# Bias weights of the sampled position bias put on diagonals of TensorE's stationary matrices

## The chip, the cores and the metric

The kernel runs on one core of a Trainium2 chip. A core has a matrix engine (TensorE, PE in the profile; PEld are its weight loads), a vector engine (VectorE, DVE), an activation engine (ScalarE, ACT), a general engine (GpSimd, POOL) and a queue engine for transfers (SyncE, SP). Each engine works through its own list of instructions in order; semaphores order them against each other. The metric is the time of one execution on the device in microseconds, the median over runs; lower is better. One further execution was taken with the hardware profiler, and durations and waits come from that one.

## The reference, cut to what matters

The reference is two layers on a tensor of 4 x 32 x 32 x 384: a deformable attention, then a linear attention with a mixture of experts. Only the deformable attention's bias and softmax matter here. With 4 batches, 6 heads of 64 channels, and n = 1024 positions, each key position has an offset, and the bias is a bilinear sample of a learned table around it:

```python
attn = jnp.einsum('bmhc,bnhc->bhmn', qh, k) * scale
disp = (ref.reshape(1, n, 1, 2) - pos.reshape(Bq * G, 1, n, 2)) * 0.5
bias = _bilinear_sample(rpe_img, disp)          # four neighbours, four weights
attn = jax.nn.softmax(attn + bias, axis=-1)
out = jnp.einsum('bhmn,bnhc->bmhc', attn, v)
# in _bilinear_sample:
top = tl + ax * (tr - tl)
bot = bl + ax * (br - bl)
out = top + ay * (bot - top)
```

For one key position the fractional parts `ax` and `ay` are the same for all 1024 queries. So the whole bias row of a key is a window of 33 x 33 values of the upsampled table, with one weight for its upper rows, one for its lower rows, one for the left columns and one for the right columns:

bias[y, x] = wl * t[y, x] + wr * t[y, x + 1], with t[y, x] = wu * win[y, x] + wd * win[y + 1, x].

## The kernel before, in words

Keys lie on the 128 partitions, queries along the free dimension. A unit is one batch and head (24 in all); its 1024 keys are 8 blocks of 128, worked two at a time. A pair of blocks is called p (96 in all, 4 per unit, `KP = 4`), its place in the unit is `p % KP`, and the blocks in the pair are e = 0 and e = 1. The loop `for g in range(NP + 7)` runs a software pipeline over pairs, with kp = g % 4; in one turn it works on several pairs at once:

- `fetch_windows` (L1168): GpSimd gathers the 128 windows of a block with an indirect transfer, for pair g + 4.
- `upper` (L1184, ScalarE) and `lower` (L1194, VectorE) make t, 128 x (32 x 33), for pair g + 2. There are four buffers for t.
- `left` (L1202, ScalarE) writes o = wl * t[:, :, 0:32], a 128 x 1024 tile, for pair g + 2.
- `scores` (L1221 and L1226, TensorE) for pair g + 1, in two steps. A step covers one half of one block and of the other. Its matmuls work on 64 x 64 tiles of the array: two tiles off the diagonal hold keys and multiply queries, two on the diagonal hold an identity and add o to the same PSUM bank group. PSUM holds one such tile ps of 128 x 2 x 1024, so the next pair's scores wait until this one has been read. Between the steps stands a small ScalarE copy (`turn_over`, L1241), which orders the second quarters behind the first.
- `right` (L1252, VectorE) for pair g + 1: for each half e, S[:, e] = wr * t[:, :, 1:33] + ps[:, e], from PSUM to SBUF.
- `running` (L1270, VectorE) keeps the running maximum over the pairs of a unit; the last pair adds a maximum of the two halves (L1272). `highest` and `spread` (L1282, L1286, L1298, L1306) turn that maximum into a row: transposes on TensorE (pm), a reduction on VectorE (nm), transposes again (pb), a copy on ScalarE (pbs).
- `minus` (L1311, VectorE) and `weights_of` (L1315, ScalarE, the exponential) for pair g - 4; `values` (L1329 and L1338, TensorE) for pair g - 5.
- `out_of` (L1354, ScalarE, kp = 0) evacuates a unit's output; `to_queries` (L1372 to L1388) and `to_channels` (L1405, L1412, in units of odd head) turn and normalise it; `project` (L1429, L1438, L1441) multiplies by the output weights, in kp = 0 and kp = 2. In the first units `last_pieces` (L257 to L295) puts what is left of the keys and values of later batches in the same places.

The order of the instructions on TensorE, ScalarE, VectorE and GpSimd in this stage is the order in which these calls are written (`tc.manual_schedule`); waits are derived from the tiles that instructions read and write. In one turn VectorE runs: running maximum (or, for kp = 0, the two `lower`), minus, the two `lower`, the two `right`. ScalarE runs: two `upper`, the copy of `turn_over`, the exponential, then the two av copies in kp = 0, then the two `left`.

Stages ahead of this one (norm, convolution, offsets, sampling, keys and values, tables) are ordered by a planner; stages after it are the linear attention and the experts. The change is in this one alone.

Of the kernel before, what the change touches and what calls it, by code (L numbers as in the profile page):

```python
# [11 lines left out]
F32 = mybir.dt.float32  # L12
I32 = mybir.dt.int32
AF = mybir.ActivationFunctionType
# [5 lines left out]
P = 128  # L20
B, HI, WI, NC = 4, 32, 32, 384
# [3 lines left out]
G, GC = 6, 64  # L25
# [126 lines left out]
def bc(ap, axis, n):  # L152

    dims = [list(d) for d in ap.ap]
    dims.insert(axis, [0, n])
    return bass.AP(ap.tensor, ap.offset, dims)
# [3 lines left out]
def body(  # L160
# [8 lines left out]
    nc = tc.nc  # L169
# [11 lines left out]
    ident = const.tile([P, P], F32, tag="ident", name="ident")  # L181
# [60 lines left out]
    x0 = early.tile([P, NB, NC], F32, tag="x0", name="xr0")  # L242
# [58 lines left out]
    with tc.tile_pool(name="a_w", bufs=1) as aw, tc.tile_pool(name="a_1", bufs=1) as a1, tc.tile_pool(  # L301
        name="a_2", bufs=2
    ) as a2, tc.tile_pool(name="a_3", bufs=2) as a3, tc.tile_pool(name="a_s", bufs=2) as asm, tc.tile_pool(
        name="a_cv", bufs=1, space=PSUM
    ) as pcv, tc.tile_pool(name="a_mm", bufs=2, space=PSUM) as pmm, tc.tile_pool(
        name="a_tr", bufs=3, space=PSUM
# [13 lines left out]
        step = plan.step  # L320
# [379 lines left out]
        os_ = {}  # L700
# [222 lines left out]
        for b in range(B):  # L923
# [56 lines left out]
            for f in range(2):  # L980
# [22 lines left out]
                for i, n in enumerate(sizes):  # L1003
                    k0, r = K4 * f + i * n, n / K4
# [109 lines left out]

    with tc.tile_pool(name="b_w", bufs=1) as bwp, tc.tile_pool(name="b_qkv", bufs=2) as bq, tc.tile_pool(
        name="b_win", bufs=4
    ) as bwin, tc.tile_pool(name="b_t", bufs=4) as bt, tc.tile_pool(name="b_o", bufs=2) as bo_, tc.tile_pool(
        name="b_s", bufs=6
    ) as bS, tc.tile_pool(name="b_m", bufs=2) as bm, tc.tile_pool(name="b_ao", bufs=1) as bao, tc.tile_pool(
        name="b_y", bufs=3  # L1120
# [2 lines left out]
        nc.sync.dma_start(wo, w_out.rearrange("(a p) d -> p a d", p=P))  # L1123
        bo = bwp.tile([P, NC], F32, tag="bo", name="bo")
        nc.sync.dma_start(bo, bc(b_out, 0, P))
        units = [(b, h) for b in range(B) for h in range(G)]
        ao = {}
        heads = {}

        HALF = [slice(e * GC, (e + 1) * GC) for e in range(2)]  # L1130
        FULL = [slice(f * 512, (f + 1) * 512) for f in range(2)]
        SYNC = mybir.DependencyInfo(mybir.DependencyClass.Sync, mybir.DependencyReason.DATA)
        KP = NB // 2
        NP = KP * len(units)

        def load_qk(u):


            b, h = u
            c, r0 = h // 2, (h % 2) * GC  # L1140
            q = bq.tile([P, N], F32, tag="q", name=f"q{b}_{h}")
            k = bq.tile([P, NB, GC], F32, tag="k", name=f"k{b}_{h}")
            ks = k_d[b][c][r0 : r0 + GC, :].rearrange("p (a e j) -> p a e j", e=2, j=GC)
            for e in range(2):
                nc.sync.dma_start(q[HALF[e], :], q_d[b][c][r0 : r0 + GC, :])
                nc.sync.dma_start(k[HALF[e]], ks[:, :, 1 - e, :])
            return q, k
# [9 lines left out]


        wins, ts, os_, pss, Ss, turns = {}, {}, {}, {}, {}, {}
        qk, vs, ms, nms, pbss, pos, avs = {}, {}, {}, {}, {}, {}, {}  # L1160

        def fetch_windows(p):
# [13 lines left out]
        def weight(p, e, i):  # L1176
            b, h = units[p // KP]
            return bw[b][:, 2 * (p % KP) + e, h, i : i + 1]
# [19 lines left out]
        def left(p, e):  # L1198

            if p < NP:  # L1200
                o = bo_.tile([P, HI, WI], F32, tag="o", name=f"o{p}_{e}")
                nc.scalar.activation(o, ts[p, e][:, :, 0:WI], AF.Copy, scale=weight(p, e, 2))  # L1202
                os_[p, e] = o.rearrange("p y x -> p (y x)")

        def scores(p, step):


            if p >= NP:
                return
            i, kp = divmod(p, KP)  # L1210
            if step == 0:
                if kp == 0:
                    qk[i] = load_qk(units[i])
                pss[p] = bps.tile([P, 2, N], F32, tag="s", name=f"ps{p}")
            q, k = qk[i]
            ps = pss[p]
            e, d = 1 - step, step
            made = []
            for f in range(2):
                for r in range(2):  # L1220
                    made.append(nc.tensor.matmul(  # L1221
                        ps[HALF[1 - r], e, FULL[f]], k[HALF[r], 2 * kp + e, :], q[HALF[r], FULL[f]],
                        start=(step == 0), stop=(step == 1),
                    ))
                for r in range(2):
                    made.append(nc.tensor.matmul(  # L1226
                        ps[HALF[r], d, FULL[f]], ident[HALF[r], HALF[r]], os_[p, d][HALF[r], FULL[f]],
                        start=(step == 0), stop=(step == 1),
                    ))
            if step == 0:  # L1230
                turns[p] = made
            else:
                for i_ in made:
                    tc.add_manual_dep(i_.ins, turns[p].ins.name, SYNC, reason="second quarters")
                del turns[p]
# [10 lines left out]
        def right(p):  # L1246

            if p < NP:
                ps = pss.pop(p)
                st = bS.tile([P, 2, N], F32, tag="S", name=f"S{p}")  # L1250
                for e in range(2):
                    nc.vector.scalar_tensor_tensor(  # L1252
                        st[:, e, :].rearrange("p (y x) -> p y x", x=WI),
                        ts.pop((p, e))[:, :, 1:WIN],
                        weight(p, e, 3),
                        ps[:, e, :].rearrange("p (y x) -> p y x", x=WI),
                        ALU.mult,
                        ALU.add,
                    )
                    del os_[p, e]  # L1260
                Ss[p] = st
# [236 lines left out]
        with tc.manual_schedule(  # L1498
# [9 lines left out]
            for p in range(2):  # L1508
                for e in range(2):
                    upper(p, e)  # L1510
                    lower(p, e)
                    if p == 0:
                        left(p, e)
                fetch_windows(p + 2)
            scores(0, 0)
            turn_over(0)
            scores(0, 1)
            for e in range(2):
                left(1, e)
            right(0)  # L1520
            for g in range(NP + 7):


                i, kp = divmod(g, KP)
                values(g - 5, 0)
                scores(g + 1, 0)
                for e in range(2):
                    upper(g + 2, e)
# [30 lines left out]
                for e in range(2):  # L1559
                    if kp:  # L1560
                        lower(g + 2, e)
                    left(g + 2, e)
                fetch_windows(g + 4)
                if kp % 2 == 0:
                    project(1)
                right(g + 1)
                if g == 15 * KP:
                    load_early()
# [7 lines left out]
            while waiting:  # L1576
                tag, n = spots.pop(0)
# [152 lines left out]
    with tc.tile_pool(name="c_1", bufs=1) as c1, tc.tile_pool(name="c_2", bufs=2) as c2, tc.tile_pool(  # L1730
        name="c_s", bufs=2
# [320 lines left out]
    with tc.tile_pool(name="d_w1", bufs=1) as dw1, tc.tile_pool(name="d_s1", bufs=1) as ds1, tc.tile_pool(  # L2052
        name="d_w2", bufs=1
    ) as dw2, tc.tile_pool(name="d_s2", bufs=1) as ds2, tc.tile_pool(name="d_2", bufs=2) as d2p, tc.tile_pool(
        name="d_h", bufs=3
# [94 lines left out]
        for t in range(-2, len(units)):  # L2150
# [12 lines left out]
            d = ds[j]  # L2163
# [59 lines left out]
```

## Time and profile before

| quantity | value |
|---|---|
| median of 3 runs | 2853.29 us (2848.89 to 2854.21) |
| the profiled execution | 2848.2 us, span of its instructions 2846.1 us |
| TensorE busy | 2586.8 us, 91% |
| VectorE busy | 1579.4 us, 55% |
| ScalarE busy | 1157.8 us, 41% |
| GpSimd busy | 855.1 us, 30% |
| mean granted TensorE clock | 0.968 of full |
| attention stage, first scores to last `right` | about 388 to 1365 us |

The shares are averages over stages with different limits: in the stage of the experts, from about 1800 us to the end, TensorE is busy nearly all the time and VectorE little; in the attention stage VectorE is the busiest. So the page's totals don't say what a change to the attention is worth; the rows of that stretch do. In the lines that follow, "x8" after a group is the number of instructions, the two figures in front are start and duration in us (timelines) or total busy us and mean ns (groups), and a bracket at the end gives the idle time before and who ended it. A float32 matmul makes two records.

### The profile page before, as it was taken

To read this page: it belongs to the slowest core of one execution; us is meant where nothing else is said; L and a number is where in the kernel's file an instruction comes from. 1 tells how busy PE (TensorE), PEld (TensorE's weight loads), DVE (VectorE), ACT (ScalarE), POOL (GpSimd) and SP (SyncE) were. 2 spreads that over 40 slices of the span, in tenths; PEclk is the share of its full clock that TensorE was granted. 3 is DMA by queue.
4 is the path that set the end of the run, shared out by engine and by line. 5 is a ranking of instruction groups with operands and counts; after the bars stand their busy time and mean duration, and the time that the engine had idled before them with its cause. 6 is when DMAs were issued, how large, how long until landed. Compare 5 with 4: busy or idle time off the path is not lost. (4 is left out here: it accounts for less than half of the span.)

```text
span 2846.1 us, 33342 instructions
## 1 busy us (share of the span) xinstructions
PE 2586.8 (91%) x12731; PEld 1283.8 (45%) x12731; DVE 1579.4 (55%) x2349; ACT 1157.8 (41%) x1532; POOL 855.1 (30%) x776
## 2 busy tenths in 40 slices
PE   8899938898989988888799898999999999999999
PEld 5455512332333333233365554555555555555566
DVE  3888859999999999999656765000101011011011
ACT  5565536777667766676323322111111111111121
POOL 1668863232333333332112335211112111021121
PEclk9899969999999999999999999999999999999999
DMA  7934575454546555544121312622223433374371
GB/s 205 257 114 132 175 208 165 130 154 146 164 145 195 176 157 149 145 151 127 55 74 51 120 45 70 250 103 103 103 103 118 147 129 140 115 255 172 117 267 59
DMA packets 267899, 404.77 MB, mean 142 GB/s; under 512 B 134674, under 2 KB 207634, under 8 KB 267356
## 3 DMA queue, kind: packets, MB, share of 16 engines
q1 hardware_dynamic: 214912, 230.43, 25.6%
q0 software_dynamic: 52112, 172.15, 18.7%
q8 instruction: 100, 1.64, 0.2%
q14 instruction: 59, 0.48, 0.1%
q10 hardware_dynamic: 716, 0.07, 0.0%
HBM read 345.68 MB, written 70.06 MB: 146 GB/s over the span
## 5 line engine op out<-in xcount | busy, mean ns | idle before, releaser
L2070 PE MATMUL ph<-d_xT,w 128*128 128x512 f32 (+1 forms) x1152 | 484.1, 554 | 1.3 <-ACT h L2077 1.3
L2102 PE MATMUL acc<-w,h 128*128 128x384 f32 x1392 | 480.3, 486 | 0.0
L1168 POOL DMA_INDIRECT win<-table,widx x192 | 280.2, 1459 | 640.3 <-DVE t L1194 608.5
L1221 PE MATMUL ps<-q,k 64*64 64x512 f32 x1536 | 382.1, 611 | 90.7 <-DVE S L1252 43.6
L2077 ACT ACTIVATE h<-ph,b1c 128x512 f32<-128x512 f32 (+1 forms) x192 | 124.1, 647 | 776.3 <-PE ph L2070 761.7
L1226 PE MATMUL ps<-o,ident 64*64 64x512 f32 x1536 | 378.4, 612 | 9.5 <-ACT o L1202 9.5
L2102 PEld LDWEIGHTS acc<-w,h 128*128 128x128 f32 x1392 | 264.1, 190 | 208.5 <-issue 73.2
L2070 PEld LDWEIGHTS ph<-d_xT,w 128*128 128x128 f32 x1152 | 217.0, 191 | 196.3 <-issue 144.5
L2132 POOL DMA_INDIRECT out<-rows,ei x67 | 67.1, 1002 | 700.2 <-DVE rows L2129 691.4
L871 POOL DMA_INDIRECT ga<-img,pidx x192 | 233.5, 1216 | 145.7 <-DVE gd L600 62.5
L1315 ACT ACTIVATE S<-S 128x2048 f32<-128x2048 f32 x96 | 183.4, 1910 | 190.3 <-DVE S L1311 190.3
L1221 PEld LDWEIGHTS ps<-q,k 64*64 64x64 f32 x1536 | 99.2, 134 | 355.4 <-issue 211.5
L1722 DVE COPY d_xT<-e_tr 128x512 f32<-128x512 f32 (+2 forms) x75 | 36.6, 512 | 386.1 <-PE e_tr L1719 386.1
L1194 DVE SCALAR_TENSOR_TENSOR t<-win,bw,t 128x1056 f32<-128x1056 f32 x192 | 244.7, 1316 | 5.9 <-ACT t L1184 4.6
L1252 DVE SCALAR_TENSOR_TENSOR S<-t,bw,ps 128x1024 f32<-128x1024 f32 x192 | 237.1, 1277 | 18.9 <-PE ps L1226 16.0
L2121 DVE SCALAR_TENSOR_TENSOR rows<-b2r,en,rows 128x384 f32<-128x384 f32 x67 | 40.9, 618 | 359.9 <-DMA rows<-out,ei 321.1
L1184 ACT ACTIVATE t<-win,bw 128x1056 f32<-128x1056 f32 x192 | 218.1, 1168 | 39.2 <-DMA win<-table,widx 38.1
L1202 ACT ACTIVATE o<-t,bw 128x1024 f32<-128x1024 f32 x192 | 212.8, 1144 | 37.0 <-DVE t L1194 30.1
L1329 PE MATMUL po<-S,v 128*64 128x512 f32 x768 | 199.1, 642 | 24.4 <-ACT av L1354 13.9
L1311 DVE TENSOR_TENSOR S<-S,pbs 128x2048 f32<-128x2048 f32 x96 | 219.0, 2283 | 2.1 <-ACT pbs L1306 2.1
L2129 DVE SCALAR_TENSOR_TENSOR rows<-acc,en,rows 128x384 f32<-128x384 f32 x67 | 41.4, 618 | 218.2 <-PE acc L2102 216.3
L1270 DVE TENSOR_TENSOR m<-m,S 128x2048 f32<-128x2048 f32 x48 | 117.1, 2440 | 1.6
(350 smaller groups left out, 3442.0 us busy)
## 6 DMA issues: line engine op xcount, KB each, us to landing
w<-in_L_ffn_w SPq DMA_DIRECT2D x50, 2304.0 KB
img<-in_x SPq DMA_DIRECT2D x48, 256.0 KB
q<-q_d SPq DMA_DIRECT2D x48, 256.0 KB
x<-in_x SPq DMA_DIRECT2D x8, 768.0 KB
q_d<-qt SPq DMA_DIRECT2D x24, 256.0 KB
v_d<-qkvw SPq DMA_DIRECT2D x32, 192.0 KB
v<-v_d SPq DMA_DIRECT2D x24, 256.0 KB
k<-k_d SPq DMA_DIRECT2D x48, 128.0 KB
```

Source lines behind the costliest of these rows:

```text
L871: nc.gpsimd.indirect_dma_start(out=ga[:, g].rearrange("p s c -> p (s c)"), out_offset=None, in_=img[b][:, :], in_offset=bass.IndirectOffse ...
L1168: nc.gpsimd.indirect_dma_start(out=win, out_offset=None, in_=tables[h // 2][:, :], in_offset=bass.IndirectOffsetOnAxis(ap=widx[b][:, nb, h ...
L1184: nc.scalar.activation(t.rearrange("p y x -> p (y x)"), wins[p, e][:, : HI * WIN], AF.Copy, scale=weight(p, e, 0),)
L1194: nc.vector.scalar_tensor_tensor(tf, wins.pop((p, e))[:, WIN:], weight(p, e, 1), tf, ALU.mult, ALU.add)
L1202: nc.scalar.activation(o, ts[p, e][:, :, 0:WI], AF.Copy, scale=weight(p, e, 2))
L1221: made.append(nc.tensor.matmul(ps[HALF[1 - r], e, FULL[f]], k[HALF[r], 2 * kp + e, :], q[HALF[r], FULL[f]], start=(step == 0), stop=(step ...
L1226: made.append(nc.tensor.matmul(ps[HALF[r], d, FULL[f]], ident[HALF[r], HALF[r]], os_[p, d][HALF[r], FULL[f]], start=(step == 0), stop=(ste ...
L1252: nc.vector.scalar_tensor_tensor(st[:, e, :].rearrange("p (y x) -> p y x", x=WI), ts.pop((p, e))[:, :, 1:WIN], weight(p, e, 3), ps[:, e, : ...
L1311: nc.vector.tensor_tensor(Ss[p], Ss[p], bc(pbss[p // KP][:, :], 1, 2), ALU.add)
L1329: nc.tensor.matmul(pos[i][0][HALF[f], :], vs[i][:, 2 * kp + e, :], Ss[p][:, e, FULL[f]], start=(first and e == 0), stop=(last and e == 1),)
L2070: nc.tensor.matmul(ph if short(d) else ph[:, :n], a, m, start=(c == 0), stop=(c == CK - 1))
L2102: nc.tensor.matmul(d["acc"][0 if short(d) else s][:, :NC], h[:, s * P : (s + 1) * P], d["w2"][:, hc, :], start=(hc == 0), stop=(hc == HC - 1),
```

## The change

The weight wl is no longer multiplied into t by ScalarE. Instead ScalarE writes a 128 x 64 tile whose diagonals (one per half of the partitions) hold wl, from a folded identity `fold`; TensorE uses that tile as the stationary matrix in place of the identity, and t itself, read with 32 columns of each row of 33, as the moving one. In two blocks of the eight of a unit (`WHOLE`: block e = 1 of the pairs 1 and 3) the right columns go the same way, with a second diagonal tile of wr and two more matmuls per half; there `right` is a plain ScalarE copy from PSUM to S instead of the VectorE instruction. The pool of the o tiles has six buffers instead of two. `fold` is made by two GpSimd copies ahead of the stage.

```diff
-        name="b_win", bufs=4 ... tc.tile_pool(name="b_o", bufs=2) as bo_
+        name="b_win", bufs=4 ... tc.tile_pool(name="b_o", bufs=6) as bo_
+        fold = bwp.tile([P, GC], F32, tag="fold", name="fold")
+        for e in range(2):
+            nc.gpsimd.tensor_copy(
+                fold[e * GC : (e + 1) * GC, :], ident[e * GC : (e + 1) * GC, e * GC : (e + 1) * GC]
+            )
+        WHOLE, rights = ((1, 1), (3, 1)), {}
         def left(p, e):
             if p < NP:
-                o = bo_.tile([P, HI, WI], F32, tag="o", name=f"o{p}_{e}")
-                nc.scalar.activation(o, ts[p, e][:, :, 0:WI], AF.Copy, scale=weight(p, e, 2))
-                os_[p, e] = o.rearrange("p y x -> p (y x)")
+                os_[p, e] = diagonal(p, e, 2)
+                if (p % KP, e) in WHOLE:
+                    rights[p, e] = diagonal(p, e, 3)
+        def diagonal(p, e, i):
+            o = bo_.tile([P, GC], F32, tag="o", name=f"o{p}_{e}_{i}")
+            nc.scalar.activation(o, fold, AF.Copy, scale=weight(p, e, i))
+            return o
+        def columns_of(p, e, r, f, x0):
+            return ts[p, e][HALF[r], 16 * f : 16 * f + 16, x0 : x0 + WI]
         def scores(p, step):
...
-                        ps[HALF[r], d, FULL[f]], ident[HALF[r], HALF[r]], os_[p, d][HALF[r], FULL[f]],
-                        start=(step == 0), stop=(step == 1),
+                        ps[HALF[r], d, FULL[f]], os_[p, d][HALF[r], :], columns_of(p, d, r, f, 0),
+                        start=(step == 0), stop=(step == 1 and (p, d) not in rights),
+                    ))
+                for r in range(2 if (p, d) in rights else 0):
+                    made.append(nc.tensor.matmul(
+                        ps[HALF[r], d, FULL[f]], rights[p, d][HALF[r], :], columns_of(p, d, r, f, 1),
+                        start=False, stop=(step == 1),
                     ))
         def right(p):
...
                 for e in range(2):
+                    if rights.pop((p, e), None) is not None:
+                        nc.scalar.copy(st[:, e, :], ps[:, e, :])
+                        del os_[p, e], ts[p, e]
+                        continue
                     nc.vector.scalar_tensor_tensor(
```

More of the change, by code (lines that the diff above doesn't have):

```diff
@@ L1116, in body @@
         name="b_win", bufs=4
-    ) as bwin, tc.tile_pool(name="b_t", bufs=4) as bt, tc.tile_pool(name="b_o", bufs=2) as bo_, tc.tile_pool(
+    ) as bwin, tc.tile_pool(name="b_t", bufs=4) as bt, tc.tile_pool(name="b_o", bufs=6) as bo_, tc.tile_pool(
         name="b_s", bufs=6
```

## The prediction

> **What bounds the kernel now.** I read the busy time by stretch first, then the groups of the attention stage, then the timelines of single iterations around the edit. Stretches (columns: PE, PEld, DVE, ACT, POOL busy us, granted clock, DMA share, GB/s):
>
> ```profile
> 460.00:1345.00 885.00, 781.87 (x5176) 278.61 (x5168) 860.88 (x614) 621.91 (x625) 278.60 (x198) 0.98 0.52 155
> ```
>
> The change touches this stage alone. VectorE is busy 861 of 885 us here, TensorE 782. The half maximum (L1272) comes once per unit, 24 times, and recurs every 40.2 us; in a typical unit VectorE is busy 39.85 of that. So VectorE sets the period, and ScalarE (70%) has room. The groups:
>
> ```profile
> L1226 PE MATMUL ps<-o,ident 64*64 64x512 f32 x1458 | 354.9, 605 | 0.0
> L1252 DVE SCALAR_TENSOR_TENSOR S<-t,bw,ps 128x1024 f32<-128x1024 f32 x182 | 224.7, 1277 | 15.6 <-PE ps L1226 12.8
> L1202 ACT ACTIVATE o<-t,bw 128x1024 f32<-128x1024 f32 x181 | 200.4, 1144 | 31.0 <-DVE t L1194 26.6 <-PE ps L1226 1.1
> L1306 ACT COPY pbs<-pb 128x1024 f32<-128x1024 f32 x22 | 21.8, 992 | 0.0
> ```
>
> L1252 (`right`) is what the change takes off VectorE in part, L1202 (`left`) what shrinks on ScalarE; L1306 has the shape of the new copy.
>
> One iteration with kp = 0, VectorE: minus (L1311), the two halves of `right`, the running maximum (L1270):
>
> ```profile
> 1340.62 2.28 DVE L1311 TENSOR_TENSOR S<-S,pbs 128x2048 f32<-128x2048 f32 x1
> 1342.83 2.46 DVE L1252 SCALAR_TENSOR_TENSOR S<-t,bw,ps 128x1024 f32<-128x1024 f32 x2
> 1345.32 2.29 DVE L1270 TENSOR_TENSOR m<-S,S 128x2048 f32<-128x2048 f32 x1
> ```
>
> ScalarE over the same time:
>
> ```profile
> 1342.94 1.91 ACT L1315 ACTIVATE S<-S 128x2048 f32<-128x2048 f32 x1 [2.99 <-DVE S L1311]
> 1344.76 1.05 ACT L1354 COPY av<-po 128x512 f32<-128x512 f32 x2
> 1345.70 2.20 ACT L1202 ACTIVATE o<-t,bw 128x1024 f32<-128x1024 f32 x2
> 1347.79 2.23 ACT L1184 ACTIVATE t<-win,bw 128x1056 f32<-128x1056 f32 x2
> ```
>
> VectorE never pauses; ScalarE starts its exponential only when minus ends, and works without a break until 1350. TensorE ended this step's scores here and went to the next product:
>
> ```profile
> 1341.91 0.60 PE L1226 MATMUL ps<-o,ident 64*64 64x512 f32 x2
> 1342.44 2.20 PE L1429 MATMUL y<-wo,ao 128*128 128x384 f32 x6
> ```
>
> An iteration with kp = 2, VectorE and then TensorE:
>
> ```profile
> 715.75 2.54 DVE L1194 SCALAR_TENSOR_TENSOR t<-win,bw,t 128x1056 f32<-128x1056 f32 x2
> 718.21 2.47 DVE L1252 SCALAR_TENSOR_TENSOR S<-t,bw,ps 128x1024 f32<-128x1024 f32 x2
> 720.71 2.84 DVE L1270 TENSOR_TENSOR m<-m,S 128x2048 f32<-128x2048 f32 x1
> ```
>
> ```profile
> 713.97 1.09 PE L1405 MATMUL pi<-ident,at 128*128 128x128 f32 x8
> 714.99 0.65 PE L1221 MATMUL ps<-q,k 64*64 64x512 f32 x2
> ...
> 716.87 2.20 PE L1429 MATMUL y<-wo,ao 128*128 128x384 f32 x6
> ...
> 725.64 1.09 PE L1282 MATMUL pm<-ident,m 128*128 128x128 f32 x8
> ```
>
> Scores end at 716.87, 1.3 us before `right` wants them: small slack.
>
> **What the Trainium skill says.** "ScalarE: Activation LUTs", What ACT_TABLE_LOAD costs: 186 ns + 0.833 ns per element, about 93 ns more per pointer operand, neighbours overlapping by about 93 ns. For 128x1024 with a pointer scale that is 1132 ns; the trace has 1144, so it holds. "TensorEngine Tiling (Array Packing)", Available Configurations: 64x64 gives four independent tiles. The trace agrees: two qk and two identity records start within 0.02 us and the next four follow 0.43 us later, the time of one full-array record here.
>
> **Part by part.** (1) `left`: 192 activations of 1144 ns become 64-element ones. By that page 186 + 53 + 93 = 332 ns, 240 ns apart: an estimate. ScalarE sheds 2 x (1.06 - 0.24) = 1.6 us per iteration. It wasn't the bound, so nothing is gained directly. (2) The identity products become diagonal products with t as moving operand, rows of 32 in a stride of 33: same count and size. The trace shows no such operand; I take no penalty. From below it can't be faster than 0.43 us per record; from above, a halved rate doubles 1.75 us of every step. (3) 48 `right` halves leave VectorE: 2 per unit, 1.235 us apart, -2.47 us. (4) Each gives two more record pairs per f on the diagonal tiles, which already work the whole step: 2 f x 2 records x 0.43 = +1.7 us on TensorE per WHOLE block (0.86 if the idle off-diagonal tiles absorb half). TensorE is 35.5 us busy per unit; 3.4 more is 38.9, just short of VectorE's 40.2. (5) 48 copies PSUM to S on ScalarE, 0.99 us by L1306. (6) `fold`: two small copies in Pool's queue, behind the last sampling gathers and ahead of the fourth window gather; in the changed order three window gathers come before the last 24 sampling gathers. First windows earlier, last gathers about 5 us later: I take zero, bounds -5 to +5 us.
>
> The point that decides is the waits of (5). In the changed program as built, the copy of half 1 waits for VectorE's `right` of half 0 (both write one S tile), and the running maximum, VectorE's next instruction after it in these iterations, waits for the copy. So the halves don't run side by side, and VectorE idles while ScalarE copies.
>
> kp = 2: VectorE saves 1.235, then waits 0.04 + 0.99 + 0.04 = 1.07: net -0.17 to -0.19. In units of odd head, the pi transposes (L1405) push the scores: they end at 716.87 + 1.7 = 718.6, plus 0.15 to VectorE, against 718.21: +0.5, net +0.34. TensorE's lateness then passes through y, values and two score steps to pm: 725.64 + 1.09 + 1.7 puts its end at 728.4, where VectorE's reduction (L1286), at 727.39 now and 0.34 later then, would want it at 727.7: about +0.6 more, in the units with a product in that place (most).
>
> kp = 0: ScalarE isn't free when half 0 ends. Behind minus stand the exponential, two av copies and two diagonals. `left` started at 1345.70 (two av copies, L1354, just ahead); from there two diagonals take 0.5, the copy 0.99, so the maximum starts at 1347.24 instead of 1345.32: +1.9. Three other units give +1.7 by the same sum (`left` at 700.94, 861.69, 1183.38, plus 1.54, against the maximum at 700.80, 861.55, 1183.23). TensorE's +1.7 hides here: scores end at 1344.15 and half 0 by 1345.6, before ScalarE is ready at 1346.2. I take +1.7.
>
> Sum: odd heads 1.7 + 0.34 + 0.6 = 2.6, even 1.7 - 0.2 = 1.5, mean 2.07; 22 units with av copies give 45.5, the first two about 2: +48 us. The profiled run took 2848.2 (span 2846.1), so 2896; the median of the runs, 5 us above it, gives 2901.
>
> **Rivals.** *VectorE really sheds the work*: if copy and half 0 ran beside each other and ScalarE were free, 48 x 1.235 = 59 us go: 2794. For it: VectorE is the bound and ScalarE gets lighter. Against: the two waits. It decides for faster only if the copy ends before 1.235 us of idle per block has gone by in kp = 0 also, so ScalarE would have to be free 1.9 us earlier there. 0.04. *Only part of the stall shows*, because later slack swallows kp = 0's (say half of 1.7, TensorE's hidden): 24 x 0.85 = 20: 2873. Against: VectorE has 0.4 us of slack in 40.2. 0.13. *TensorE becomes the bound*: its 3.4 us per unit reach the period on top of the unavoidable wait for nm (1.9 us at L1298) and part of the copy's: 24 x 3.4 = 82: 2935. For: 38.9 busy and waits that can't be filled. 0.17. *Strided t streams at half rate*: four score pairs per unit each 3.5 us longer, more than 24 x 12 = 290 us: over 3140. Nothing in the trace for it: 0.03. *No net change*, costs and saving cancelling as at kp = 2 alone: 2853. 0.03.
>
> **How the numbers follow.** The copy-wait case has 0.60, its own range 2884 to 2918 (kp = 0 at 1.4 to 2.3, pm's wait 0 or 1, start -5 to +5). Rivals of one sign lie either side, so the range runs 2872 to 2938. About 0.2% is what a measurement here can tell from no change. Faster 0.04, within 0.2% 0.03, slower 0.93.
>
> **What would show it.** Right: period of L1272's line 42 to 42.6 us; VectorE idle before the running maximum, ended by ScalarE's copy of S, about 3 us in kp = 0 and 1.1 in kp = 2; its busy time down by 2.5 per unit; `right` waiting for the scores in odd heads only; diagonals of 0.3 us; diagonal records still 0.43 apart. Wrong: VectorE running on without those waits; TensorE busy nearly all the unit; score records further apart than 0.43 us.

## The result and the profile after

The changed kernel takes 2922.55 us (median of 4 runs, 2915.70 to 2925.28) against 2853.75 for the kernel before on the same chip: a ratio of 1.0235, with a 95% interval of 1.0219 to 1.025. It is slower by 69 us, where +48 was predicted. The profiled run took 2920.75 us with a span of 2919.0, so its span is 72.9 us longer than that of before (2846.1).

First, the stretch of the attention after the change (columns as before: PE, PEld, DVE, ACT, POOL busy, granted clock, DMA share, GB/s):

```profile
480.00:1400.00 920.00, 829.73 (x5442) 292.24 (x5442) 798.49 (x564) 528.25 (x702) 278.32 (x198) 1.00 0.49 148
```

VectorE, busy 97% of this stretch before, is busy 87% now, and TensorE 90%: no engine is busy all the time any more, and VectorE waits for others. The groups in the same stretch:

```profile
L1243 PE MATMUL ps<-t,o 64*64 64x512 f32 x1382 | 341.3, 602 | 0.0
L1278 DVE SCALAR_TENSOR_TENSOR S<-t,bw,ps 128x1024 f32<-128x1024 f32 x131 | 163.5, 1276 | 44.5 <-PE ps L1248 40.6 <-PE ps L1243 3.8
L1248 PE MATMUL ps<-t,o 64*64 64x512 f32 x344 | 88.1, 589 | 0.0
L1215 ACT ACTIVATE o<-fold,bw 128x64 f32<-128x64 f32 x215 | 59.9, 336 | 0.0
L1275 ACT COPY S<-ps 128x1024 f32<-128x1024 f32 x43 | 43.4, 1009 | 31.7 <-DVE S L1278 31.7
```

The diagonal products (L1243) last what the identity products did (602 against 605 ns), and a diagonal takes 336 ns. `right` (L1278) now waits for the extra products (L1248), and the copy (L1275) waits for VectorE's half of `right`. VectorE's waits, before and then after (columns: who waits and for whom; us in total, times, longest):

```profile
DVE nm L1286 <- PE pm L1282: 8.3, 10, 2.2
DVE S L1252 <- PE ps L1226: 8.1, 10, 1.3
```

```profile
DVE m L1296 <- ACT S L1275: 50.8, 43, 1.5
DVE S L1278 <- PE ps L1248: 40.6, 31, 1.8
DVE nm L1312 <- PE pm L1308: 22.8, 16, 3.5
```

16 us of waits over 22.0 units have become 118 us over 21.6, with the 3.8 us that the group of `right` adds: 0.75 us per unit have become 5.46. So VectorE sheds about 2.3 us of work per unit (860.88 us in 22.0 units are 39.2, 798.49 in 21.6 are 36.9) and waits 4.7 us more. The half maximum, once per unit, shows the sum; first before, then after (24 of them; durations, then the first and the last start):

```profile
L1272 DVE TENSOR_TENSOR m<-m x24: 1224/1225/1227, 439.6 to 1366.3; 128x1024 f32<-128x1024 f32 x24
```

```profile
L1298 DVE TENSOR_TENSOR m<-m x24: 1224/1225/1226, 452.5 to 1430.9; 128x1024 f32<-128x1024 f32 x24
```

From the first to the last are 23 periods: (1366.3 - 439.6) / 23 = 40.29 us before, 42.54 after. That cuts the 72.9 us in three: **+12.9 at the first half maximum**, **23 x 2.25 = +51.7 in the stage**, and **+8.3 after the last one**. "The period" below is always this quotient.

Of the 12.9 us, 4.6 were there before the order of GpSimd's instructions first differs. The last sampling gather that has the same place in both orders (the 168th of 192) starts at 363.3 us here and at 358.7 before; in the other profiles of the first group of runs below it lies between 358.0 and 363.6, so this is probably the scatter of single executions. From that gather to the first half maximum it is 80.9 us before and 89.2 after: 8.3 us (by chance the same figure as after the last one) belong to the start of the stage. Without the 4.6 the profiles differ by 68.3 us, as the medians do (69).

One iteration with kp = 0 after, on VectorE, on ScalarE and on TensorE:

```profile
892.21 2.28 DVE L1337 TENSOR_TENSOR S<-S,pbs 128x2048 f32<-128x2048 f32 x1
896.32 1.28 DVE L1278 SCALAR_TENSOR_TENSOR S<-t,bw,ps 128x1024 f32<-128x1024 f32 x1 [1.82 <-PE ps L1248]
898.82 2.29 DVE L1296 TENSOR_TENSOR m<-S,S 128x2048 f32<-128x2048 f32 x1 [1.22 <-ACT S L1275]
```

```profile
894.53 1.91 ACT L1341 ACTIVATE S<-S 128x2048 f32<-128x2048 f32 x1 [2.54 <-DVE S L1337]
896.35 1.05 ACT L1380 COPY av<-po 128x512 f32<-128x512 f32 x2
897.29 0.59 ACT L1215 ACTIVATE o<-fold,bw 128x64 f32<-128x64 f32 x2
897.78 1.00 ACT L1275 COPY S<-ps 128x1024 f32<-128x1024 f32 x1
```

```profile
892.61 0.65 PE L1238 MATMUL ps<-q,k 64*64 64x512 f32 x2
...
893.53 0.59 PE L1248 MATMUL ps<-t,o 64*64 64x512 f32 x2
894.39 1.02 PE L1243 MATMUL ps<-t,o 64*64 64x512 f32 x4
895.25 1.02 PE L1248 MATMUL ps<-t,o 64*64 64x512 f32 x4
896.20 2.20 PE L1455 MATMUL y<-wo,ao 128*128 128x384 f32 x6
```

VectorE finishes minus at about 894.5 and waits 1.82 us, until TensorE has the scores of this WHOLE block at 896.2. Then comes half 0 of `right`, then the copy, and VectorE waits 1.22 us more for it. The scores' step runs from 892.61 to 896.20, 3.59 us; a step without a WHOLE block takes 1.88 (889.73 to 891.61 just before). The products with the keys (L1238) are over by 894.5, and the two diagonal tiles work on alone. In kp = 2 it is the same pair of waits, with the first one small; behind it VectorE's reduction waits for pm, which TensorE reaches late:

```profile
916.64 1.28 DVE L1278 SCALAR_TENSOR_TENSOR S<-t,bw,ps 128x1024 f32<-128x1024 f32 x1 [0.20 <-PE ps L1248]
919.06 2.29 DVE L1296 TENSOR_TENSOR m<-m,S 128x2048 f32<-128x2048 f32 x1 [1.13 <-ACT S L1275]
927.04 1.23 DVE L1312 TENSOR_REDUCE nm<-pm 128x8 f32<-128x1024 f32 x1 [2.23 <-PE pm L1308]
```

The start of the stage after, from ScalarE's, TensorE's and GpSimd's timelines:

```profile
368.84 1.17 ACT L1192 ACTIVATE t<-win,bw 128x1056 f32<-128x1056 f32 x1 [17.98 <-DMA win<-table,widx]
409.96 0.35 ACT L1215 ACTIVATE o<-fold,bw 128x64 f32<-128x64 f32 x1 [25.05 <-POOL fold L1129]
```

```profile
370.64 8.76 PE L286 MATMUL psv<-qkvw,xT 128*128 128x384 f32 x18 [16.00 <-ACT kt L279]
```

```profile
409.69 0.23 POOL L1129 COPY fold<-ident 64x64 f32<-64x64 f32 x1 [6.25 <-DMA ga<-img,pidx]
```

Three window gathers now go ahead of the last sampling gathers. The first `upper` (L1192), which waits for a window, stands in ScalarE's queue ahead of the evacuations that TensorE needs (L279), so both lose 16 to 18 us; and `fold`, last in GpSimd's queue behind the sampling gathers, whose landing its second half waits for, is done at 409.9, where ScalarE has waited 25 us for it. The first diagonal product starts at 410.36, the first identity product did at 402.64.

### The profile page after: what moved, and what is told of

Its sections match the earlier page's. It is cut to its first block, busy times and chain, and to the rows that moved or that the text cites. A ratio compares the mean times of both kernels' runs of the same rounds, so it can differ in the third digit from the quotient of the medians.

```text
span 2919.0 us, 33972 instructions
## 1 busy us (share of the span) xinstructions
PE 2665.4 (91%) x13115; PEld 1308.1 (45%) x13115; DVE 1522.7 (52%) x2301; ACT 1060.7 (36%) x1628; POOL 857.8 (29%) x778
## 5 line engine op out<-in xcount | busy, mean ns | idle before, releaser
L1238 PE MATMUL ps<-q,k 64*64 64x512 f32 x1536 | 380.4, 611 | 91.9 <-DVE S L1278 62.1
L1243 PE MATMUL ps<-t,o 64*64 64x512 f32 x1536 | 385.8, 611 | 0.9 <-ACT o L1215 0.9
L1192 ACT ACTIVATE t<-win,bw 128x1056 f32<-128x1056 f32 x192 | 220.9, 1176 | 133.7 <-DVE S L1278 110.9
L1202 DVE SCALAR_TENSOR_TENSOR t<-win,bw,t 128x1056 f32<-128x1056 f32 x192 | 245.3, 1316 | 20.1 <-ACT t L1192 18.9
L1238 PEld LDWEIGHTS ps<-q,k 64*64 64x64 f32 x1536 | 94.8, 134 | 354.7 <-issue 174.4
L1278 DVE SCALAR_TENSOR_TENSOR S<-t,bw,ps 128x1024 f32<-128x1024 f32 x144 | 179.8, 1276 | 59.5 <-PE ps L1248 55.5
L1355 PE MATMUL po<-S,v 128*64 128x512 f32 x768 | 188.9, 613 | 6.9 <-ACT S L1341 3.8
L2155 DVE SCALAR_TENSOR_TENSOR rows<-acc,en,rows 128x384 f32<-128x384 f32 x67 | 41.4, 618 | 219.3 <-PE acc L2128 217.7
L1881 POOL DMA_INDIRECT tab_d<-ent,si x64 | 65.3, 1021 | 162.6 <-DVE selw L1876 140.0
```

The source lines that it names most:

```text
L1192: nc.scalar.activation(t.rearrange("p y x -> p (y x)"), wins[p, e][:, : HI * WIN], AF.Copy, scale=weight(p, e, 0),)
L1202: nc.vector.scalar_tensor_tensor(tf, wins.pop((p, e))[:, WIN:], weight(p, e, 1), tf, ALU.mult, ALU.add)
L1238: made.append(nc.tensor.matmul(ps[HALF[1 - r], e, FULL[f]], k[HALF[r], 2 * kp + e, :], q[HALF[r], FULL[f]], start=(step == 0), stop=(step ...
L1243: made.append(nc.tensor.matmul(ps[HALF[r], d, FULL[f]], os_[p, d][HALF[r], :], columns_of(p, d, r, f, 0), start=(step == 0), stop=(step == ...
L1278: nc.vector.scalar_tensor_tensor(st[:, e, :].rearrange("p (y x) -> p y x", x=WI), ts.pop((p, e))[:, :, 1:WIN], weight(p, e, 3), ps[:, e, : ...
L1355: nc.tensor.matmul(pos[i][0][HALF[f], :], vs[i][:, 2 * kp + e, :], Ss[p][:, e, FULL[f]], start=(first and e == 0), stop=(last and e == 1),)
```

## The experiments

The questions are three: is the new operand dear; which of the two waits costs the 2.25 us per unit; and what are the 21 us outside the stage? They were run in three groups at different times, the second on another chip, each with its own runs of the kernel before (medians 2854.54, 2914.9 and 2897.15); so only ratios and periods are compared across groups. In the profiles the longer times of the second and third group lie ahead of the stage. Typical units aren't slower there: they recur every 40.2 us before, and also in each group's kernel without the costs of the WHOLE blocks.

**Diagonals without whole blocks.**

```diff
-        WHOLE, rights = ((1, 1), (3, 1)), {}
+        WHOLE, rights = (), {}
```

> The changed kernel with no WHOLE block: left columns on diagonals, all right columns on VectorE as before, fold where the change put it. My theory: diagonals with a strided moving operand cost nothing, the period of a unit stays 40.2 to 40.4 us, and only the later start of the stage (first half maximum 12.9 us later in the changed kernel, of it about 8 before the first scores) remains: 2861 to 2866 us. Rival (strided operand or small diagonals cost time): period over 41 us, 2880 us or more. Rival (the start is noise of one profile): 2853 us.

Measured: 2862.40 us, ratio 1.0026 (1.0019 to 1.0034); period 40.24 against 40.29; VectorE waits 8.4 us at `right` and 8.2 at nm, as before. So the strided operand and the diagonals cost nothing in the stage, and the ScalarE time they free brings nothing. The 7.9 us lie outside, as expected: in the profile the first half maximum is at 442.9 (+3.3), and 8.0 more go after the last one.

**`fold` made early.** The two copies go to the start of the program, where GpSimd has nothing else in its queue:

```diff
     nc.gpsimd.memset(token, 0.0)
+    fold = ab.tile([P, GC], F32, tag="fold", name="fold")
+    for e in range(2):
+        nc.gpsimd.tensor_copy(
+            fold[e * GC : (e + 1) * GC, :], ident[e * GC : (e + 1) * GC, e * GC : (e + 1) * GC]
+        )
...
-        fold = bwp.tile([P, GC], F32, tag="fold", name="fold")
...
```

> The changed kernel with fold made at the kernel's beginning in an earlier pool, so that GpSimd's order of sampling and window gathers is as before the change. Theory (fold's place held up keys, values, gathers and the first scores): 8 to 13 us less than the changed kernel, 2910 to 2915 us, period of a unit still 42.5 us. Rival (the start's shift comes from the WHOLE blocks of unit 0): within 3 us of the changed kernel, 2920 us or more.

Measured: 2915.63 us, ratio 1.0214 (1.0195 to 1.0233), 7 us below the changed kernel; its first half maximum starts at 439.1, as before's does (439.6), and its period is 42.57. The time is 0.6 us above the range that was expected. So the place of `fold` is what delays the start, by 7 us in the medians. Counted from the 168th sampling gather, the first half maximum comes after 79.3 us here, 80.9 before, and with `fold` late after 84.9 us in the run of the diagonals alone and 89.2 in the changed kernel. The stage is untouched by it.

**Without the extra products.** The copies stay, the right columns of the WHOLE blocks are left out:

```diff
-                        start=(step == 0), stop=(step == 1 and (p, d) not in rights),
+                        start=(step == 0), stop=(step == 1),
...
-                for r in range(2 if (p, d) in rights else 0):
+                for r in range(0):
```

> The changed kernel without the extra products of the right columns in the WHOLE blocks (their right columns are left out of the bias), copies on ScalarE kept. Theory of two overlapping causes: in kp = 0 ScalarE's chain takes the place of TensorE's lateness, so only about 0.7 us per unit goes (the reduction's wait for pm and part of kp = 2): 2900 to 2908 us. Rival TensorE alone: the stage's loss of 2.25 us per unit goes, and the time is that of the diagonals alone, about 2865 us. Rival copy wait alone: no change, 2920 us.

Measured: 2892.25 us, ratio 1.0129 (1.0111 to 1.0147), period 41.50. That is 8 us below the lower end of what was expected, and neither rival's value. VectorE's waits in this run, and one kp = 0 of it:

```profile
DVE m L1296 <- ACT S L1275: 90.5, 45, 3.1
DVE nm L1312 <- PE pm L1308: 8.0, 10, 2.1
DVE S L1278 <- PE ps L1243: 1.0, 1, 1.0
```

```profile
922.35 2.29 DVE L1296 TENSOR_TENSOR m<-S,S 128x2048 f32<-128x2048 f32 x1 [2.91 <-ACT S L1275]
```

The 40 us at `right` are gone, and 40 us have come up at the running maximum: with the scores early, half 0 ends early, and VectorE waits 2.91 us in kp = 0 for a ScalarE that is still at its exponential, its av copies and its diagonals. So in kp = 0 the two delays lie beside each other, and ScalarE's alone makes nearly all of it (2.91 of 3.04 us). What did go is most of the reduction's wait for pm (22.8 to 8.0) and about 1 us per unit in all.

**The copy on VectorE.** The products stay, the copy moves:

```diff
-                        nc.scalar.copy(st[:, e, :], ps[:, e, :])
+                        nc.vector.tensor_copy(st[:, e, :], ps[:, e, :])
```

> The changed kernel with the WHOLE blocks' copies from PSUM on VectorE in place of ScalarE, extra products kept. Theory of two overlapping causes: VectorE's waits for the copy go (2.35 us per unit) but it does the copies itself (about 1.1 to 1.2 us each, 2.3 per unit), and TensorE's lateness stays: within 8 us of the changed kernel, 2912 to 2926 us. Rival copy wait alone: the loss is the wait less the copy, so also near the changed kernel, but right then no longer waits for the scores. Rival TensorE alone: same time, with the wait of right for the scores near 2 us per unit as before.

Measured: 2918.39 us, ratio 1.0218 (1.0199 to 1.0238), period 42.46. VectorE's waits and its copy:

```profile
DVE S L1278 <- PE ps L1248: 40.6, 31, 1.8
DVE nm L1312 <- PE pm L1308: 22.4, 16, 3.5
```

```profile
L1275 DVE COPY S<-ps x48: 1212/1218/1221, 432.0 to 1425.8; 128x1024 f32<-128x1024 f32 x48
```

The wait for the copy is gone, but the copy takes 1218 ns on VectorE, hardly less than the `right` it replaces (1277 ns). So this kernel does VectorE's old work again plus the waits for TensorE. The shift to ScalarE saves a VectorE instruction and costs a wait as long: 2.35 us of waiting per unit (1.22 + 1.13) against 2.44 of copying. In kp = 0 TensorE's delay alone, 1.82 us and then the copy, makes the same sum.

**Both: no extra products, copy on VectorE.** Both edits at once; again the right columns are left out.

> The changed kernel without the extra products (right columns of the WHOLE blocks left out of the bias) and with the WHOLE blocks' copies on VectorE. If the two waits are all of the stage's loss, VectorE is the bound again at its work of before less 48 x 0.06 us: period 40.1 to 40.2 us, time within 4 us of the diagonals alone, 2858 to 2864 us. Each edit by itself gave 1.04 and 0.08 us per unit; together they must give 2.3 to 2.4. Rival (a third cost in the WHOLE blocks, such as the second diagonal or the evacuation of PSUM): 2875 us or more.

Measured: 2921.76 us, ratio 1.0026 (1.0004 to 1.0049); the half maximum gives a period of 40.16:

```profile
L1298 DVE TENSOR_TENSOR m<-m x24: 1224/1224/1226, 495.0 to 1418.8; 128x1024 f32<-128x1024 f32 x24
```

VectorE waits 6.7 us at `right` and 8.3 at nm in 22 units. That is the stage of before. Taken out alone the extra products are worth 1.04 us per unit and the copy's place 0.08, taken out together 2.38. So these two account for all of the stage's loss, and the copy's place seems free as long as TensorE's delay is there: with the products gone, moving the copy brings 1.34 us per unit.

**One WHOLE block, that of pair 1** (whose `right` comes in kp = 0):

```diff
-        WHOLE, rights = ((1, 1), (3, 1)), {}
+        WHOLE, rights = ((1, 1),), {}
```

> The changed kernel with one WHOLE block per unit, pair 1 alone, whose evacuation falls in kp = 0 behind the exponential and the av copies. By the layout of the measured durations this place costs about 1.7 us per unit and the other (pair 3) 0.5: period 42.0 us, 2901 to 2908 us with the late start. Rival (both places cost alike, half each): period 41.4 us, about 2890 us.

Measured: 2967.63 us, ratio 1.017 (1.0112 to 1.0228), period 41.80. The ratio can't tell the two theories apart: the times expected on the first chip are ratios of 1.0166 to 1.019, and 1.013 for the rival. By the period, expected at 42.0 by the theory and 41.4 by its rival, it lies between, nearer the theory. VectorE's waits (in a stretch that takes in the end of the first unit, with its 5.9 us):

```profile
DVE S L1278 <- PE ps L1248: 44.0, 21, 5.9
DVE m L1296 <- ACT S L1275: 25.3, 21, 1.2
```

Nearly all of the wait for TensorE belongs to pair 1, in kp = 0: one wait per unit here, 44.0 us in 21, for 40.6 us in 31 waits with both blocks. About two thirds of the 2.25 us come from pair 1 (1.5 us), the rest from pair 3; each period is of one profile.

**One WHOLE block, half 0 of pair 0.** If the two waits are the cause, a WHOLE block must gain time where neither applies. `right` of pair 0 comes in kp = 3, where no running maximum follows, and with e = 0 the copy is first: half 1 waits for it, and VectorE has nm and `lower` (L1202) to do meanwhile. The products of this block would push the transposes of the maximum (pm), which stood behind them on TensorE; these go ahead of the scores. `fold` is early, too.

```diff
-        WHOLE, rights = ((1, 1), (3, 1)), {}
+        WHOLE, rights = ((0, 0),), {}
...
+                if kp == KP - 1:
+                    highest(i, 0)
                 scores(g + 1, 1)
                 if kp == 0:
                     out_of(g - 5)
                 elif kp == KP - 1:
-                    highest(i, 0)
                     highest(i, 1)
```

> One WHOLE block per unit at pair 0, half e = 0, evacuated in kp = 3, where the scores end 5 us before VectorE wants them and no av copy stands on ScalarE; the transposes of the maximum (pm) moved ahead of the second score step of kp = 3; fold made early. The copy should end before VectorE reaches its half, so VectorE sheds 1.24 us per unit with no wait: period about 39.0 us, 24 x 1.24 = 30 us less than before the change, 2820 to 2828 us. Rival (VectorE's shed work comes back as a wait wherever the block stands, or the moved transposes hold up the scores): 2850 us or more.

Measured: 2888.00 us, ratio 0.9904 (0.987 to 0.9939), period 38.73 (39.0 was expected): faster than before by 1% or 27 us, where 30 were forecast.

**The kernel before with only pm moved** (the same move of `highest(i, 0)`), as a control:

> The kernel before with only the transposes of the maximum moved ahead of the second score step of kp = 3, the control for the previous run: VectorE stays the bound with the same work, so 2843 to 2854 us, at most the few tenths of a us per unit that its reduction waited for pm. Rival (the move itself is worth the gain of the previous run): 2830 us or less.

Measured: 2921.09 us, ratio 1.0008 (0.9987 to 1.0029), period 40.69. Moving pm alone brings nothing. VectorE's wait for pm nearly goes (0.3 us in 22 units, for 8.3), but its waits for the scores at `right` rise from 8.1 to 30.2 us: the transposes now stand ahead of these.

**With the old pool size.** All kernels so far with the small o pool ended 8 to 13 us later after the last half maximum, and the control, with the old pool, 0.8. One suspect was `bqs` (VectorE's scaling of a bias for the next stage). It stood beside the last half maximum before. In the diagonals-only run it stands behind the last values and waits for TensorE; the shifted memory is the likely reason, since in no kernel with the old pool size does it stand there:

```profile
1366.23 0.16 DVE L1743 TENSOR_SCALAR bqs<-cols 128x3 f32<-128x3 f32 x1
```

```profile
1397.99 0.17 DVE L1769 TENSOR_SCALAR bqs<-cols 128x3 f32<-128x3 f32 x1 [1.85 <-PE po L1364]
```

In the third group an unused tile keeps the o pool at its old size, and `fold` is early; one kernel with no WHOLE block, one with the two of the change, one with pair 0's:

```diff
+        pad = bo_.tile([P, 2 * N - 6 * GC], F32, tag="pad", bufs=1, name="pad")
```

> Diagonals alone (no WHOLE block) with fold made early and the pool of the o tiles padded to its size of before, so that what is laid out after it lies where it lay before. If fold's place and the shifted memory are all that the diagonals alone cost (7.9 us in the run of the diagonals alone), this equals the kernel before: ratio 0.998 to 1.001. Rival (the diagonals or the strided operand cost something themselves): 1.002 or more.

> The changed kernel with fold early and the pool of the o tiles padded to its size of before. Only the stage's own loss should be left: 23 x 2.27 us per unit, about 52 us, ratio 1.018 to 1.020 against 1.0235 of the changed kernel; VectorE's scaling of the query bias no longer stands in the layer norm waiting for the last values. Rival (the later 8 us are not from the layout): within 3 us of the run with fold early, ratio 1.021.

> The run with the WHOLE block at pair 0, half 0, plus the padded pool. About 8 us less than that run: ratio to the kernel before 0.986 to 0.989. Rival: the same as that run, 0.990.

Diagonals only: 2891.22 us, ratio 0.9982 (0.9967 to 0.9998), period 40.26, first half maximum to end as before (0.3 us longer after the last one). The whole change: 2950.79 us, ratio 1.0185 (1.0167 to 1.0204), period 42.53. Pair 0: 2859.15 us, ratio 0.9874 (0.9853 to 0.9895), the best of all and faster than both kernels, with a period of 38.79:

```profile
L1299 DVE TENSOR_TENSOR m<-m x24: 1224/1224/1226, 477.3 to 1369.5; 128x1024 f32<-128x1024 f32 x24
```

So with `fold` early and the memory as before, the change still costs 1.85%. But `bqs` isn't the whole cause: in the second of these kernels it is beside the running maximum again (at 1465.31), and yet the time from the last half maximum to the end is 9.2 us longer than before's; in the third it is 3.1 us longer. What goes along with the loss in every profile is a wait of TensorE. These are its transposes of the next stage's layer norm (c_tr) and of the last unit's output (pi), before, after, and in the whole change with the old pool size:

```profile
1395.84 0.55 PE L1487 MATMUL c_tr<-ident,c_ln 128*128 128x128 f32 x3 [0.28 <-DVE c_ln L1105]
1400.07 1.04 PE L1405 MATMUL pi<-ident,at 128*128 128x128 f32 x8
```

```profile
1460.41 0.55 PE L1513 MATMUL c_tr<-ident,c_ln 128*128 128x128 f32 x3 [1.79 <-DVE c_ln L1105]
1466.79 1.81 PE L1431 MATMUL pi<-ident,at 128*128 128x128 f32 x8
```

```profile
1497.75 0.55 PE L1514 MATMUL c_tr<-ident,c_ln 128*128 128x128 f32 x3 [1.79 <-DVE c_ln L1110]
1503.86 1.91 PE L1432 MATMUL pi<-ident,at 128*128 128x128 f32 x8
```

The fourteen profiles fall into two groups. In the nine that lose 8 to 13 us, TensorE waits 1.8 us for this layer norm, and the clock granted from 29 to 37 us after the last half maximum is 0.60 to 0.78. In the five that lose at most 3.6 us it waits 0.28 us or less, and the clock is 0.94 to 1.00. The wait comes about in two ways: `bqs` makes the layer norm 1.6 us late (six kernels), or TensorE is through with its last values 1.5 us earlier and waits for a layer norm on time (the changed kernel, the one without extra products, and the whole change with the old pool size). In the changed kernel 2.9 us are lost by the time of the next products (y) and another 3 or so where VectorE waits 3.94 us for a transfer of the layer norm's input (at 1504.7), a wait that before doesn't have. No run changes TensorE's wait alone, so that it brings the low clock is not shown, and the rest of the 8 us stays open.

The best kernel in kp = 3, ScalarE and then VectorE:

```profile
948.39 1.01 ACT L1276 COPY S<-ps 128x1024 f32<-128x1024 f32 x1 [0.58 <-PE ps L1244]
```

```profile
946.43 1.22 DVE L1313 TENSOR_REDUCE nm<-pm 128x8 f32<-128x1024 f32 x1 [1.04 <-PE pm L1309]
947.57 2.54 DVE L1203 SCALAR_TENSOR_TENSOR t<-win,bw,t 128x1056 f32<-128x1056 f32 x2
950.02 1.27 DVE L1279 SCALAR_TENSOR_TENSOR S<-t,bw,ps 128x1024 f32<-128x1024 f32 x1
```

The copy runs from 948.39 to 949.40 beside VectorE's two `lower`, and half 1 of `right` starts at 950.02 without a wait. One `right` per unit, 1.2 us of busy time, is really shed. Typical units recur every 39.0 us for 40.2; the mean falls by 1.5 us because the first period is shorter still (35.7 for 38.9).

**The same without pm moved:**

> The previous kernel with the transposes of the maximum left behind the second score step. The layout of the measured durations says that the extra 1.7 us on TensorE then comes between VectorE's maximum and its reduction, and eats the 1.24 us that VectorE sheds: 0.2 to 0.5 us per unit slower than before, ratio 1.000 to 1.004. Rival (the place of the block alone matters): ratio as in the previous run, 0.989 or less.

Measured: 2896.91 us, ratio 0.9997 (0.9982 to 1.0013), period 40.48. VectorE's wait for pm, with pm moved and then without:

```profile
DVE nm L1313 <- PE pm L1309: 6.6, 10, 2.1
```

```profile
DVE nm L1313 <- PE pm L1309: 36.3, 21, 3.9
```

Unmoved, the block's extra products delay pm and the whole gain goes into that wait, 36.3 us in place of 6.6 in some 21 units each. The time is just at the lower end of what was expected (1.000). The move is worth nothing alone and everything here: it is the order on TensorE that decides whether VectorE's saving counts.

## Why the prediction was right, and where it was not

Direction and mechanism were right: VectorE gives up work and gets more waiting. The time, 2922.55, is 21 us above the predicted 2901. That is inside the stated range, but 5 us above the range of the copy-wait case by itself (2884 to 2918), so the width that was kept for the rivals held it. The stage came out within 4 us of its sum; most of the 21 us lie at its start and after it. By the prediction's steps:

1. *Diagonals* (1): 332 ns and 240 apart was estimated from the price in the Trainium skill, "ScalarE: Activation LUTs", What ACT_TABLE_LOAD costs; measured 336 and about 240. That ScalarE's saving gains nothing is shown by the diagonals-only run (period 40.24).
2. *Strided operand* (2): no penalty, right: 602 ns against 605, and records 0.43 us apart.
3. *VectorE's saving* (3): -2.3 us of busy time per unit, where -2.47 was reckoned.
4. *Extra products* (4): 1.7 us per WHOLE block, measured 3.59 - 1.88 = 1.71, from the upper of the two bounds. The off-diagonal tiles absorb nothing of it; they finish early and stand idle.
5. *The copy's waits* (5): right in sum. kp = 0 was put at 3 us of idle before the running maximum; only 1.22 us stand there, ended by ScalarE's copy, and 1.82 stand before `right`, ended by TensorE, 3.04 together. kp = 2 was put at 1.1 and has 1.13. Less the 1.235 saved, kp = 0 comes to +1.8 (predicted +1.7). Typical periods alternate between 42.8 us, where VectorE waits for the pm that an odd head has delayed, and 41.9, for 42.8 and 41.7 by the prediction's +2.6 and +1.5. The mean came out at 2.25 for 2.07, because single units with other late work reach 45.4.
   One statement in it failed: "TensorE's +1.7 hides here". It doesn't hide, it ties. `right` waits for the scores in kp = 0 too, not in odd heads alone, and only the remainder is the ScalarE chain. The prediction's own times held this: scores until 1344.15, with minus over by 1342.9. The sum is the same since both delays end at nearly one time (half 0 at 897.6, ScalarE's diagonals at 897.9), which is in part luck; but for mending it matters, as the two runs that take one of them out show (1.04 and 0.08 us per unit, for 2.38 with both).
6. *`fold` and the gathers* (6): this is the term of the sum that was mis-sized. "I take zero, bounds -5 to +5 us": it costs 7 us by the medians and 8.3 of the 12.9 us in the profile, and with `fold` early it is gone. The last sampling gather starts 9.1 us later than before (401.2 for 392.1; 4.6 of it from before the orders differ), where 5 was reckoned. The prediction saw that three window gathers would come before the last sampling gathers, and saw `fold` behind them, but set the later gathers off against the earlier windows. It did not ask who stands behind them: the first `upper` holds up ScalarE's evacuations, these TensorE's products, and the first diagonals wait for `fold`. Which of these makes how much of the 7 us, the runs don't separate.
7. *After the attention*: the prediction had no term for it, and the span lost 8.3 us there. It goes along with a wait of TensorE and a lower clock behind it; the cause isn't shown.

So of the 24.9 us that the profiled span lost beyond the predicted 48, 8.3 are step 6, 4.6 were there ahead of it, 8.3 are outside the sum, and the stage itself, 51.7 for 47.5, gives some 4. Of the rivals, "TensorE becomes the bound" (2935) is nearer in time than the prediction itself, and half right: 67 of VectorE's 118 us of waits end with TensorE. But TensorE is late without being full: it is busy 38.4 of 42.5 us per unit, and without its extra products the period is still 41.50. "VectorE really sheds the work" failed by the two waits that were held against it, and came true in pair 0, where they don't apply.

## What to carry to other kernels

Taking an instruction off the bounding engine pays only if what replaces it ends before that engine next wants its result: look at the instruction right behind it there, and at what stands ahead of the replacement in its new queue. Where two delays end at the same time, removing one shows little; take out both before judging either. And when a small set-up step joins a queue, ask who waits behind it as well as what it waits for.

## What the runs showed of the hardware

A plain copy of 128x1024 float32 from PSUM on VectorE took 1218 ns, only 59 ns less than the multiply-add with a third operand (1277); on ScalarE it took 1009. Extra products on two of the four 64x64 tiles lengthened the step by their full 1.71 us: the other two tiles' products ran beside the first of them and were over 1.7 us before the step's end. And after a wait of TensorE of 1.8 us at the end of the attention the clock granted over the following 8 us was 0.60 to 0.78 in nine profiles, where it was 0.94 to 1.00 in five with a wait of at most 0.28 us; the same eight 128x128 transposes took 1.81 and 1.91 us in two of the nine, and 1.04 in one of the five. That the wait brings the lower clock is not shown.
